# A deformable convolution, attention and experts in one kernel: each image's offset convolutions move among its own sampling steps, and two expert tiles are loaded earlier

## The chip, the cores and the metric

The kernel is one launch on one core of a Trainium2 chip. A core has five engines that run their own instruction streams: TensorE (PE, matrix products), VectorE (DVE), ScalarE (ACT), GpSimd (POOL) and SyncE (SP, which here only issues transfers). Sixteen DMA engines move data between device memory and the core's SBUF, and the products land in PSUM. The metric is the device time of the launch in microseconds.

## The reference, cut to what matters

The input is four images of 256 channels and 64 x 64 pixels, all in float32. The computation is

```
x = x + deform_conv(group_norm(x))       # 3 x 3, modulated, offsets from a convolution
t = tokens(x)                            # 4 x 4096 tokens of 256
t = t + attention(layer_norm(t))         # 8 heads; 4 images attend to each other
t = t + experts(layer_norm(t))           # 8 experts, the best 2 for each token
```

In the deformable convolution, a 3 x 3 convolution over the normalised image gives 27 numbers for each pixel: for each of the nine taps a shift in y, a shift in x, and a mask before its sigmoid:

```
om = conv(x, w_off) + b_off;  off = om[:18];  mask = sigmoid(om[18:])
y, x = pixel + tap + off
sampled = sum over 4 neighbours of (weight of the neighbour) * img[neighbour] * mask
out = sum over 9 taps and channels of w_conv * sampled
```

This convolution is called the offset convolution below, and the arithmetic that turns its 27 numbers into a row index and four weights for each tap is called the positions.

## The kernel before, in words

**The sampling loop** is the first stage. An image is 32 rows of 128 pixels, and each row has nine taps, so an image has 288 steps and the loop has 1,152. For each image there is a table in device memory in which one row of 4 KB holds the four neighbours of a place. In step n, an indirect transfer (`gather`, L626, issued by POOL) brings 128 such rows into one of ten buffers, ten steps ahead. `corner0` (L643, ACT) takes the first neighbour times its weight, `corner` (L651, DVE) adds the other three, `turned` (L665, PE) transposes the sum, `to_sbuf` (L671, ACT) copies it out of PSUM and `product` (L690, PE) multiplies it with the tap's weights. A row's nine taps gather in one PSUM bank; `done` (L699, L701) copies it out and stores four rows at a time. The gathers are issued in pairs, and each pair waits for the last corner sum that still reads one of its buffers.

**The preparation of an image** is cut into small pieces by `pieces(b)`, and each piece has a step number at which it is issued. The loop issues, after its own instructions of step n, what is due at n (`todo`). On DVE, ACT, PE and POOL the order of issue is the order in the program, so a piece stands exactly between two steps; SP's order is chosen by the framework. The pieces are:

- group norm: 16 statistics (L332) at steps 32 to 47 and a few small operations, done at step 56.
- `block(q, at)`, for each of eight blocks of 512 pixels. `norm` (L395) normalises the block. With `table`, `turn` and `leave` (L402, L415, L421) transpose it and store it into the table. With `offsets`, `rows_of` (L433) makes six products, `shifted` (L445) copies them with the bias, `summed` (L454) adds the three shifted rows up and `kept` (L463) copies the 27 numbers out. With both, one normalised tile, of the block and a row above and below it, serves both.
- `positions` (L509 to L556), 16 DVE pieces and one mask on ACT.

Image 0 is prepared before the loop, except for the offset convolutions and positions of blocks 2 to 7. Those stand among image 0's own steps, at 12 + 36 (q - 2), two positions a step, and are done 17 steps before the gathers need them. Images 1 to 3 are prepared in whole during the image before: the eight blocks with table and offsets come every 22 steps (`PERIOD`) from step 56, and then one set of positions over all 32 rows, one operation a step, at steps 235 to 250.

**Memory.** The stages share SBUF through pools that are opened and closed in turn. A tile that lies where an earlier one lay waits for the last use of the earlier one. The two input images in use are `a_x0` and `a_x1`, side by side; the temporaries of the positions are in `a_tmp`.

**The attention** follows in two passes over the eight blocks. In the second, `block(j)` (L1291 on), the order on all engines but POOL is written out by hand, and `chore` slips in the loading of the experts' weights (`experts_in`), the plan of the experts' tiles (`plan`) and their padding rows (`fill`). The tokens are scattered to the experts' rows in device memory as they become ready. The states of blocks 0 to 4 lie in one tile, `early_state`; when those blocks are done, the experts' weights take 10,256 of its 20,480 columns.

**The experts** follow: 142 tiles of 256 tokens. `fetch(n)` reads the tile's first row from the plan into a register of SP and loads the tile into one of five buffers `xt`; `turned_in` (L1556) transposes it on PE, `hidden` (L1577) and `result` (L1595) are the two products, and `weights1` and `weights2` copy the expert's weights. Three tiles are fetched ahead. The `xt` buffers lie where the tiles of the attention's second pass lay.

Of the kernel before, what the change touches and what calls it, by code (L numbers as in the profile page):

```python
# [17 lines left out]
P = 128  # L18
# [3 lines left out]
K2 = 9  # L22
# [23 lines left out]
EARLY = 2  # L46
PERIOD = 22
# [22 lines left out]
XTS, YS = 5, 4  # L70
NG = B * NT
# [7 lines left out]
def conv_attn_moe_kernel(  # L79
# [145 lines left out]
    with ExitStack() as actx:  # L225
# [10 lines left out]
            actx.enter_context(tc.tile_pool(name=f"a_x{i}", bufs=1)) for i in range(2)  # L236
# [80 lines left out]
        def pieces(b):  # L317
# [49 lines left out]
            om = atmp.tile([P, NR, NOFF], F32, name=f"om{b}", tag="om") if b else None  # L367

            def block(q, at, table=True, offsets=True, alone=False):
# [89 lines left out]
                def kept():  # L459
                    of[q] = om[:, rows_in(q), :] if b else atmp.tile(  # L460
                        [P, NT, NOFF], F32, name=f"om{b}_{q}", tag="om_", bufs=2
                    )
                    V.tensor_copy(of[q], t["pt"])  # L463
# [110 lines left out]
            if b:  # L574
                for q in range(NBLK):
                    block(q, n + q * PERIOD)
                n += (NBLK - 1) * PERIOD + 25
                later.append((n - 1, place_for))
                later.extend(positions(slice(0, NR), lambda: om, n, 1))
                assert n + 16 <= STEPS - AHEAD, n  # L580
                return later
# [3 lines left out]
            place_for()  # L585
            for q in range(NBLK):
                first.extend(block(q, n + 10 * q, offsets=False, alone=True))
            n += 10 * NBLK + 8
            for q in range(EARLY):
                at = n + 20 * q  # L590
                first.extend(block(q, at, table=False, alone=True))
                first.extend(positions(rows_in(q), lambda q=q: of[q], at + 25, 4))
            router = routed(
                [wconv_sb[:, ch, k, :] for ch in range(NCH) for k in range(K2)],
                wconv_sb[:, :, :, C:], rwc_sb, ps_tp, ps_om, asm, "wconv",
            )
            for m in range(NCH * K2 + 2):
                first.append((n + 10 + 1.5 * m, lambda: next(router)))
            for q in range(EARLY, NBLK):
                at = (q - 2) * NT * K2 + 12  # L600
                block(q, at, table=False)
                later.extend(positions(rows_in(q), lambda q=q: of[q], at + 25, 2))
                assert at + 33 <= q * NT * K2 - AHEAD, q
# [1189 lines left out]
```

## Time and profile before

| | us |
|---|---|
| median of three runs | 3588.42 |
| lowest and highest run | 3581.35, 3590.16 |
| the profiled execution | 3621.63 |
| its span, first to last instruction | 3619.9 |
| sampling of image 0, 1, 2 (first L671 to first L671) | 522.9, 504.9, 506.6 |
| sampling of image 3 | 512.9 |
| attention, both passes | 791.0 |
| experts and output | 701.0 |

| image | TensorE busy | DVE | ACT | POOL | granted clock | DMA share | GB/s |
|---|---|---|---|---|---|---|---|
| 0 | 468.5 | 392.4 | 291.2 | 306.5 | 0.95 | 0.90 | 320 |
| 1 | 438.1 | 376.4 | 270.5 | 324.8 | 0.94 | 0.92 | 339 |
| 2 | 437.9 | 376.6 | 269.9 | 330.4 | 0.95 | 0.91 | 331 |
| 3 | 402.5 | 354.2 | 231.9 | 345.4 | 0.88 | 0.83 | 297 |

Busy times are microseconds within the image's stretch. The clock is the share of full speed that TensorE was granted; the DMA share is the mean busy share of the sixteen DMA engines. A line of the timeline has the start, the length, the engine, the line of the kernel, the operation, what it writes and reads, a count of instructions merged into it, and in brackets how long the engine stood idle before it and what ended that. In a table of windows the last three columns are the clock, the DMA share and the rate.

### The profile page before, as it was taken

What the parts mean: (1) busy time and instruction counts of PE and PEld (TensorE: products, weight loads), DVE (VectorE), ACT (ScalarE), POOL (GpSimd) and SP (SyncE); (2) the same over time, 40 slices, a digit from 0 to 9 for tenths busy, and PEclk for the clock granted to TensorE, in tenths of its full rate; (3) what the DMA queues carried; (4) which work ended last, traced back from release to release, by engine and by line L of the source; (5) the groups of instructions that cost most, each with busy time, mean ns of one, the idle gap of its engine ahead of it and who ended that gap; (6) DMA issues with size and microseconds to landing.
All of it is one profiled execution on the core that took longest, in us unless ns stands there. A gap on an engine that the chain in (4) does not pass through costs nothing.

```text
span 3619.9 us, 49496 instructions
## 1 busy us (share of the span) xinstructions
PE 3041.8 (84%) x13658; PEld 2230.4 (62%) x13658; DVE 2480.5 (69%) x6303; ACT 1832.4 (51%) x4281; POOL 1961.6 (54%) x1818
## 2 busy tenths in 40 slices
PE   5899997899987899977777889997676588899996
PEld 4667665667665676656566655543343367788884
DVE  5867686777776777866666758875445555455887
ACT  2556554456554565544444457744344254455663
POOL 2555565666576665677666643305445536655441
PEclk8999998999998999989888989998788789999996
DMA  9889889899989899988787878723234334444888
GB/s 301 306 304 336 316 326 351 278 353 366 348 313 350 307 346 341 352 297 310 280 312 285 320 205 141 139 74 121 99 105 154 111 97 132 154 138 153 289 280 285
DMA packets 349897, 911.66 MB, mean 252 GB/s; under 512 B 43540, under 2 KB 123035, under 8 KB 347576
## 3 DMA queue, kind: packets, MB, share of 16 engines
q0 software_dynamic: 208704, 689.10, 55.1%
q1 hardware_dynamic: 140920, 219.39, 19.0%
q8 instruction: 113, 1.85, 0.2%
q14 instruction: 160, 1.31, 0.1%
HBM read 741.87 MB, written 170.12 MB: 252 GB/s over the span
## 4 chain that ended last, share of the span: by engine, by line
PE 48%; issue 14%; POOL 11%; DMA 9%; DVE 8%; another core or an unknown queue 6%; ACT 3%; SPq 0%; POOLq 0%; DVEq 0%; ACTq 0%
PE acc L690 13%; POOL g L626 10%; DMA g<-table,idx 6%; PE ph L1577 6%; PE py L1595 5%; PE tps L665 3%; PE po L433 3%; PE po L1129 3%; DVE s L651 3%; PE p_wq_sb L796 3%; PE p_wk_sb L796 3%; PE pg L796 2%; PE pv L796 1%; DVE mix L1098 1%
## 5 line engine op out<-in xcount | busy, mean ns | idle before, releaser
L651 DVE SCALAR_TENSOR_TENSOR s<-g,wts,s 128x256 f32<-128x256 f32 x3456 | 1433.5, 479 | 542.3 <-ACT s L643 374.3
L626 POOL DMA_INDIRECT g<-table,idx x1152 | 1310.4, 1137 | 765.7 <-DVE s L651 465.2
L690 PE MATMUL acc<-wconv_sb,sT 128*128 128x265 f32 x4608 | 1338.9, 415 | 274.3 <-ACT sT L671 165.7
L690 PEld LDWEIGHTS acc<-wconv_sb,sT 128*128 128x128 f32 x4608 | 832.4, 201 | 423.5 <-ACT sT L671 196.2
L671 ACT COPY sT<-tps 128x256 f32<-128x256 f32 x1152 | 425.4, 369 | 781.0 <-PE tps L665 489.9
L643 ACT ACTIVATE s<-g,wts 128x256 f32<-128x256 f32 x1152 | 588.9, 511 | 210.2 <-DMA g<-table,idx 180.9
L665 PE MATMUL tps<-ident,s 128*128 128x128 f32 x2304 | 461.7, 283 | 39.8 <-DVE s L651 37.8
L665 PEld LDWEIGHTS tps<-ident,s 128*128 128x128 f32 x2304 | 327.7, 148 | 270.1 <-issue 162.4
L1606 POOL DMA_INDIRECT ys_rows<-y,to x284 | 282.9, 996 | 299.9 <-DVE y L1603 225.2
L1577 PE MATMUL ph<-xT,w 128*128 128x256 f32 x1136 | 282.8, 392 | 35.6 <-DVE second L1563 18.3
L1273 POOL DMA_INDIRECT xs_rows<-u,slots x256 | 250.0, 976 | 94.6 <-issue 88.8
L1595 PE MATMUL py<-w,hT 128*128 128x256 f32 x1136 | 270.7, 381 | 0.0
L1581 ACT ACTIVATE hT<-ph,w 128x256 f32<-128x256 f32 x284 | 132.7, 474 | 237.2 <-PE ph L1577 170.0
L1577 PEld LDWEIGHTS ph<-xT,w 128*128 128x128 f32 x1136 | 210.3, 196 | 66.6 <-ACT hT L1581 18.4
L1600 DVE TENSOR_TENSOR y<-py,w 128x512 f32<-128x512 f32 x142 | 98.2, 691 | 206.8 <-ACT w L1539 70.7
L1595 PEld LDWEIGHTS py<-w,hT 128*128 128x128 f32 x1136 | 218.3, 192 | 30.5
L1098 DVE SCALAR_TENSOR_TENSOR mix<-pv,att,mix 128x512 f32<-128x512 f32 x192 | 131.0, 742 | 142.6 <-remote 106.3
L1103 ACT ACTIVATE gate<-pg,bg_c 128x512 f32<-128x512 f32 x64 | 43.8, 688 | 277.1 <-DVE mix L1118 190.1
L919 DVE SCALAR_TENSOR_TENSOR junk<-q,k 128x512 f32<-128x512 f32 x256 | 162.1, 687 | 24.6 <-ACT k L900 24.4
L433 PE MATMUL po<-xs,woff_sb 128*96 128x512 f32 x288 | 152.4, 612 | 0.0
L796 PE MATMUL pg<-early_state,wg_sb 128*128 128x512 f32 x160 | 87.1, 680 | 76.9 <-DVE mix L1098 61.8
L1178 POOL TENSOR_TENSOR rstd<-l3var,nhalf 128x8 f32<-128x8 f32 x16 | 26.5, 1656 | 215.1 <-DVE l3var L1176 207.2
(264 smaller groups left out, 3432.1 us busy)
## 6 DMA issues: line engine op xcount, KB each, us to landing
xt<-xs_rows SPq DMA_DIRECT2D x142, 260.0 KB
table<-zt SPq DMA_DIRECT2D x96, 256.0 KB
yk<-ys_rows SPq DMA_DIRECT2D x80, 256.0 KB
g<-table,idx POOLq DMA_INDIRECT x1152
t<-o SPq DMA_DIRECT2D x32, 530.0 KB
t<-bo_sb POOLq DMA_DIRECT2D x32, 530.0 KB
dt<-t SPq DMA_DIRECT2D x64, 265.0 KB
xraw<-in_x SPq DMA_DIRECT2D x16, 1024.0 KB
```

Source lines behind the costliest of these rows:

```text
L433: T.matmul(t["po"], woff_sb[:, ch, ki].rearrange("p kj o -> p (kj o)"), t["xs"][:, ch, ki : ki + RB], start=(n == 0), stop=(n == NCH * 3 - 1),
L626: g = G.indirect_dma_start(out=gs[n % NGB], out_offset=None, in_=tables[b], in_offset=bass.IndirectOffsetOnAxis(ap=params[b][0][:, r, k : ...
L643: first = S.activation(ss[n], gs[n % NGB][:, :C], AF.Copy, scale=params[b][1][:, 0, r, k : k + 1])
L651: last_corner[n] = V.scalar_tensor_tensor(ss[n], gs[n % NGB][:, c * C : (c + 1) * C], params[b][1][:, c, r, k : k + 1], ss[n], ALU.mult, A ...
L665: T.transpose(tps[n][:, ch * P : (ch + 1) * P], s[:, ch * P : (ch + 1) * P], ident)
L671: S.copy(sTs[n], tps.pop(n))
L690: T.matmul(accs[n // K2][:, :CR], sT[:, ch * P : (ch + 1) * P], wconv_sb[:, ch, k, :], start=False, stop=(k == K2 - 1 and ch == NCH - 1),)
L796: T.matmul(ps, w[:, ci, ch * P : (ch + 1) * P], src[:, ci, :], start=(ci == 0), stop=(ci == NCH - 1),)
L1273: s = G.indirect_dma_start(out=rows_, out_offset=bass.IndirectOffsetOnAxis(ap=slots[:, k, n : n + 1], axis=0), in_=u[:, n % NT, :], in_off ...
L1577: T.matmul(ph, w1_sb[:, ch, f * P : (f + 1) * P], xT[:, ch, :], start=(ch == 0), stop=(ch == NCH - 1),)
L1595: T.matmul(py[:, i, :], hT[:, f, i * P : (i + 1) * P], w2_sb[:, f, :], start=(f == 0), stop=(f == NCH - 1),)
L1606: s = G.indirect_dma_start(out=ys_rows[g], out_offset=bass.IndirectOffsetOnAxis(ap=to[:, i : i + 1], axis=0), in_=y[:, i, :], in_offset=No ...
```

## The change

For images 1 to 3 the preparation during the image before keeps the group norm, the eight table blocks (still every 22 steps from 56) and, of the offset convolutions, only those of blocks 0 and 1, at steps 212 and 232 (`EARLY_AT`), each followed by its own positions. The offset convolutions and positions of blocks 2 to 7 stand among the image's own steps, as those of image 0 did already. So a table block and an offset block no longer share a normalised tile, and the tile for all 32 rows' 27 numbers is gone. One of the two input images now lies at the other end of SBUF.

In the experts, `fetch` is defined inside the attention's second pass. The first two tiles are fetched there, after the last block, into the columns of `early_state` behind the weights; the other tiles use `xt` as before.

```diff
+EARLY_AT = 212
+SOONER = 2
-            actx.enter_context(tc.tile_pool(name=f"a_x{i}", bufs=1)) for i in range(2)
+            actx.enter_context(tc.tile_pool(name=f"a_x{i}", bufs=1, side=("left", "right")[i]))
+            for i in range(2)
...
-            om = atmp.tile([P, NR, NOFF], F32, name=f"om{b}", tag="om") if b else None
...
-            if b:
-                for q in range(NBLK):
-                    block(q, n + q * PERIOD)
-                n += (NBLK - 1) * PERIOD + 25
-                later.append((n - 1, place_for))
-                later.extend(positions(slice(0, NR), lambda: om, n, 1))
+            else:
+                later.append((n - 1, place_for))
+                for q in range(NBLK):
+                    block(q, n + q * PERIOD, offsets=False)
+                for q in range(EARLY):
+                    at = EARLY_AT + 20 * q
+                    block(q, at, table=False)
+                    later.extend(positions(rows_in(q), lambda q=q: of[q], at + 25, 2))
             for q in range(EARLY, NBLK):
                 at = (q - 2) * NT * K2 + 12
+                at += STEPS if b else 0
                 block(q, at, table=False)
                 later.extend(positions(rows_in(q), lambda q=q: of[q], at + 25, 2))
...
+        def fetch(n):
+            g, q = tiles[n]
+            row = nc.sync.value_load(plans[g][1][0:1, q : q + 1], min_val=0, max_val=NE * CAP)
+            if n < SOONER:
+                at = NE * WROW + n * NTB * ROW
+                xts[n] = early_state[:, at : at + NTB * ROW].rearrange("p (t c) -> p t c", c=ROW)
+            else:
+                xts[n] = mt.tile([P, NTB, ROW], F32, name=f"xt{n}", tag="xt", bufs=XTS)
...
         while chores:
             chore()
+        for n in range(SOONER):
+            fetch(n)
...
-        for n in range(FETCH):
+        for n in range(SOONER, FETCH):
             fetch(n)
```

## The prediction

> **What bounds the kernel now.** I read the slices of the page first, to see which resource is full in which stage; then the stages by the count of sampling steps; then the timeline inside one slow and one quick stretch; then the hand-over to the experts. The sampling loop fills some 2,050 us of the span of 3,619.9 us, and the first 23 of the page's 40 slices:
>
> ```profile
> PEclk8999998999998999989888989998788789999996
> DMA  9889889899989899988787878723234334444888
> GB/s 301 306 304 336 316 326 351 278 353 366 348 313 350 307 346 341 352 297 310 280 312 285 320 205 141 139 74 121 99 105 154 111 97 132 154 138 153 289 280 285
> ```
>
> The DMA engines are nearly full there and the rate swings between 278 and 366 GB/s. Every step gathers 128 rows of 4 KB, 0.524 MB, so the loop is a gather loop, and a stage at 300 GB/s is losing something. Which stages lose is seen by counting steps: L671 (the copy of a sampled tile out of PSUM) runs once a step, so its count in a window is the number of steps. Columns: window, length, busy time of L671 with its count, granted TensorE clock, DMA share, GB/s.
>
> ```profile
> 212.50:475.60 263.10, 53.31 (x144) 0.97 0.92 325
> ...
> 534.00:603.50 69.50, 13.31 (x36) 0.83 0.84 303
> ...
> 739.90:977.70 237.80, 53.40 (x144) 1.00 0.97 358
> ...
> 1034.10:1108.40 74.30, 13.13 (x36) 0.79 0.84 313
> ...
> 1239.90:1483.70 243.80, 53.46 (x144) 0.99 0.96 348
> ...
> 1540.60:1615.00 74.40, 13.21 (x36) 0.85 0.82 299
> ...
> 1630.90:2021.00 390.10, 78.33 (x213) 0.87 0.84 299
> ```
>
> In order: steps 72 to 216 and the last 36 of image 0; the same two of image 1; the same two of image 2; steps 12 to 225 of image 3. Length over count is the pace: 1.83, 1.93; 1.65, 2.06; 1.69, 2.07; 1.83 us a step. Image 3 has no preparation work left beside its steps, and yet it is slower than images 1 and 2, which prepare a whole image beside theirs. The timeline says why. First the end of image 1's whole-image position work, then the middle of image 3:
>
> ```profile
> 1032.68 9.58 DVE L651 SCALAR_TENSOR_TENSOR s<-g,wts,s 128x256 f32<-128x256 f32 x24
> 1033.89 9.20 POOL L626 DMA_INDIRECT g<-table,idx  x1 [0.30 <-issue]
> ...
> 1729.94 11.97 DVE L651 SCALAR_TENSOR_TENSOR s<-g,wts,s 128x256 f32<-128x256 f32 x30 [0.22 <-ACT s L643]
> ...
> 1733.93 7.61 POOL L626 DMA_INDIRECT g<-table,idx  x1 [0.30 <-issue]
> 1741.85 0.95 POOL L626 DMA_INDIRECT g<-table,idx  x1 [0.30 <-issue]
> ...
> 1745.59 0.88 DVE L651 SCALAR_TENSOR_TENSOR s<-g,wts,s 128x256 f32<-128x256 f32 x2 [3.68 <-ACT s L643]
> ```
>
> A gather's issue takes 0.95 us, but 9.20 and 7.61 us when the VectorE runs its corner sums without a gap, 24 or 30 in a row; it ends when the row of sums ends. Meanwhile no new transfer starts, the buffers empty, and the VectorE then sits idle (3.68 us) for data that was issued late. Ten landed buffers make the next row of sums without a gap, and so it repeats. Steps that are held up a little by other work (a convolution on TensorE) leave gaps, and the gathers go out evenly: 358 GB/s.
>
> [...]
>
> **The change, part by part.** The sums are made against the profiled execution: 3,621.63 us, span 3,619.9. The median of the runs is 3,588.42, a factor of 0.991, with which I scale at the end.
>
> Durations come from these groups of the loop (busy, mean ns, then idle before):
>
> ```profile
> L433 PE MATMUL po<-xs,woff_sb 128*96 128x512 f32 x288 | 152.4, 612 | 0.0
> ...
> L454 PE MATMUL pt<-tap_sum,oc 96*128 96x27 f32 x256 | 34.6, 257 | 1.9 <-ACT oc L445 1.8
> ...
> L395 ACT ACTIVATE xs<-xraw,nb,rs 128x640 f32<-128x640 f32 x36 | 33.4, 926 | 0.0
> ...
> L509 DVE TENSOR_TENSOR pos<-om,grid 128x576 f32<-128x576 f32 x3 | 2.3, 751 | 0.0
> ...
> L509 DVE TENSOR_TENSOR pos<-om,grid 128x72 f32<-128x72 f32 x8 | 1.8, 226 | 0.1
> ```
>
> *Convolutions moved.* Thirty of the 32 blocks run inside the loop before and after, but as 14, 8, 8, 0 in images 0 to 3 before and 8, 8, 8, 6 after. One block is twelve L433 records at a pitch of 0.43 us (5.2 us) and eight of L454 (1.0 us): 6.2 us of TensorE. Image 0 sheds six (37 us of TensorE work), image 3 takes six, and within images 1 and 2 they come every 36 steps plus two at steps 212 and 232, where they came every 22.
>
> - Image 0, steps 72 to 216: its 263.1 us become the pace of images 1 and 2 there, 1.65 or 1.69. I take 1.69: -20 us. Bounds: 0 (stays at 1.83) and -26.
> - Images 1 and 2, steps 72 to 216: 481.6 us at 1.67 go to 1.69, +5 us, since the convolutions are sparser. A block with its bias copies, sums and positions occupies 24 of 36 steps, against 16 of 22 now, so the cover is nearly as dense (67% against 73%). Bounds: 0 and +46 (all at image 3's present 1.83).
> - Image 3, steps 12 to 225: 390.1 us at 1.83. What remains to be moved is 0.539 MB a step (a gather and the output rows), 1.51 us at 358 GB/s. I take 1.69, about the middle of 1.83 and 1.51: -30 us. Bounds: -68 and, if the six blocks simply lengthen the path, +37.
>
> *Whole-image positions removed.* Sixteen steps of images 0 to 2 each carried one operation on all 32 rows, 9.0 us of VectorE an image, and the gather of 9.2 us came right after them. The last 36 steps take 69.5, 74.3 and 74.4 us; at image 3's uncovered pace of 1.83 they would take 65.9 each: -21 us. Bounds 0 and -36 (1.69).
>
> *Operations added.* Twenty-one more sets of 17 small operations on VectorE: 24 blocks at 3.6 us (the 17 small groups sum to 28.5 us for eight blocks) less 27 us, +58 us over 864 steps, 0.07 us a step. VectorE is busy 354 of 513 us in image 3 and 376 of 505 in image 1: I cost it at nothing; without that cover it is 58 us. ScalarE gets 48 more normalisations at some 0.81 us (926 ns for 640 elements, 869 for 576, taken on to 512) and 21 masks: 44 us, on an engine busy 232 to 291 us an image. Behind each stand one corner product, issued three steps ahead, and one copy; at most 0.9 us late, covered by that lead.
>
> *Queues.* Six memsets of border rows move in POOL's order from steps 56 and 210 to 212 and 192; the readers they wait for ended four steps earlier, so no gather waits. On SP five weight loads move from the end of image 2 to behind the 24th output store of image 3 and wait for the last temporaries (step 225); the next store behind them is at step 253, and their reader at the end of the loop. Nothing.
>
> *First two tiles of the experts.* The hand-over now:
>
> ```profile
> 2917.95 0.69 DVE L1146 TENSOR_TENSOR st<-po,dt 128x512 f32<-128x512 f32 x1 [0.94 <-PE po L1129]
> 2918.91 4.86 SPq L1531 DMA_DIRECT2D xt<-xs_rows  x5
> ...
> 2922.24 2.10 PE L1556 MATMUL tpx<-ident,xt 128*128 128x128 f32 x8 [4.33 <-DMA xt<-xs_rows]
> ...
> 2924.16 3.49 PE L1577 MATMUL ph<-xT,w 128*128 128x256 f32 x8
> ```
>
> SP waits 6.0 us for the last L1147 because the tile buffers lie under attention's. In state space long free the two loads go at once, some 6 us earlier; TensorE transposes at about 2918. The next thing is then ScalarE's copy of the first weights (2920.07, 0.65 us): L1577 starts at 2920.8 instead of 2924.16, -3.4 us; I take -3. Tile 2 keeps its present issue at 2918.9 and lands about 2922.2, before it is needed.
>
> Sum: -20 + 5 - 30 - 21 - 3 = -69 us: a span near 3,551; scaled, 3588.42 - 68 = 3,520 us.
>
> **Rivals.** *Nothing gained, work only moved.* If the convolutions lengthen the path wherever they stand, image 3 pays 37, image 0 gets back at most 22 (its pace can't pass image 1's), the last steps give 21 and the tiles 3: -9 us, 3,579. For it: in image 3 TensorE already takes part in long waits. Against it: images 1 and 2 carry eight blocks at a better pace than image 3 with none. *Slower: sparse cover doesn't break the rows of sums.* Between two blocks 12 steps are bare, and a row of sums needs about ten steps to shut the gathers out. If that returns every 36 steps, all the covered stretches, 645 steps and 1,134.8 us now, run at 1.83: +46; and if the last 36 steps gain nothing either, with -3: +43 us, 3,631; with their gain, 3,610. It decides from a mean pace of 1.796 us a step up (1,134.8 + 24 over 645). *Faster than I say:* if the gathers run evenly to the end, image 3 goes to 1.51 (-68), image 0 gets -26, the last steps -36: about -130 us, 3,460.
>
> **From this to the numbers.** Two times within 0.3% I can't tell apart here. Chances: my forecast, between -35 and -100 us, 0.62; the faster case, 0.12; work only moved, 0.14, whose -9 us lie near the bound of 11 and which I split 0.05 faster and 0.09 the same; slower, 0.12, of which 0.02 stay within the bound. That gives faster 0.79, same 0.11, slower 0.10. The range 3,465 to 3,590 reaches from most of the faster case to the case of moved work and leaves the slower one out; the forecast's own range is 3,488 to 3,553.
>
> **What would show it.** Right: image 3's steps 12 to 225 near 1.69 us with over 320 GB/s and a clock over 0.93; gathers over 2 us there down from a dozen to half; image 0 near 490 us; no gather of 9 us after step 250 of images 0 to 2; the first L1577 about 3 us after the last L1146. Wrong: images 1 and 2 above 1.75 us a step between 72 and 216, or the gathers of image 3 as long as now beside TensorE rows that are merely longer.

## The result, and the profile after

The changed kernel takes 3,642.69 us (median of four runs, 3,633.57 to 3,644.8), the kernel before 3,589.29: a ratio of 1.0124, 95% interval 1.0089 to 1.016. It is slower by some 53 us, where I forecast 69 us less.

The two profiled executions are nearer to each other than the medians: 3,644.8 us (span 3,643.1) against 3,621.63 (span 3,619.9). The one of before ran 32 us over its median, so the stretches below are read for their pattern, and a second pair, further down, has to confirm it.

First the same three rows of slices of the page. The changed kernel no longer has the slices of 353 and 366 GB/s in image 1 (slices 9 and 10), and image 3 (slices 18 to 23) gains little:

```profile
PEclk8999999999998999988999899999778889999996
DMA  9898899898989898988888878724325334444888
GB/s 306 310 320 317 318 327 345 306 327 321 319 321 350 301 328 312 335 307 289 308 297 308 310 236 149 140 55 146 115 79 163 120 97 132 149 141 145 292 282 288
```

Then the same stretches, counted by the copy of a sampled tile (now L675). Columns: window, length, busy time with the count of steps, clock, DMA share, GB/s.

```profile
206.70:475.20 268.50, 52.95 (x145) 0.94 0.89 318
538.30:603.90 65.60, 13.25 (x36) 0.90 0.88 327
730.80:994.80 264.00, 52.96 (x144) 0.93 0.91 323
1058.50:1122.00 63.50, 13.34 (x37) 0.87 0.89 336
1256.40:1517.50 261.10, 53.07 (x144) 0.95 0.91 326
1581.20:1643.40 62.20, 13.24 (x36) 0.89 0.80 295
1672.00:2046.30 374.30, 78.39 (x213) 0.93 0.86 305
```

The middle of images 1 and 2 went from 237.8 and 243.8 us to 264.0 and 261.1, at 323 and 326 GB/s instead of 358 and 348. The last 36 steps of images 0 to 2 and the middle of image 3 are quicker. So the gains that were expected are partly there, and a loss of 43.5 us in images 1 and 2, which was priced at 5, outweighs them, together with 18.9 us in steps 216 to 252, which were not priced at all (the table further down has every stretch).

What is new in images 1 and 2 is seen in the timeline of image 1, at the end of a block's positions (L526 is the last of them; L655 is the corner sums, L630 the gathers):

```profile
746.99 0.94 POOL L630 DMA_INDIRECT g<-table,idx  x1 [2.32 <-DVE s L655]
747.03 0.19 DVE L526 TENSOR_TENSOR wts<-hi,lo 128x36 f32<-128x36 f32 x1
747.14 0.19 DVE L526 TENSOR_TENSOR wts<-lo 128x36 f32<-128x36 f32 x1
747.24 6.03 DVE L655 SCALAR_TENSOR_TENSOR s<-g,wts,s 128x256 f32<-128x256 f32 x15
...
748.24 1.10 POOL L630 DMA_INDIRECT g<-table,idx  x1 [0.30 <-issue]
...
749.64 4.45 POOL L630 DMA_INDIRECT g<-table,idx  x1 [0.30 <-DVE s L655]
...
753.69 1.28 DVE L655 SCALAR_TENSOR_TENSOR s<-g,wts,s 128x256 f32<-128x256 f32 x3 [0.42 <-ACT s L647]
```

Two position operations a step, with no convolution beside them, put VectorE behind ScalarE: over the 24 sets of blocks 2 to 7, a step's first sum starts a median of 0.69 us after ScalarE's product for it has ended, and 0.03 us in the eight steps before a set. When the set ends, VectorE catches up in one unbroken row of 15 sums (6.03 us): within it a step's first sum starts up to 1.11 us after its product, at the step behind it 0.04 us. The third gather of that row takes 4.45 us and ends 0.82 us behind the row's last sum, near the 0.95 us of an undisturbed gather. The same stands at a fixed place behind every set: of the 144 gathers of each such stretch (gather n is that of step n, and is issued ten steps before it), numbers 91, 127, 163 and 199 of an image (or the neighbour) take 4.4 to 5.9 us, in images 0, 1 and 3 all four, in image 2 three. Before, none of the 288 in images 1 and 2 took over 2.5 us. I call those over 2.5 us late.

What it costs is in the groups of instructions of that window alone (steps 72 to 216 of image 1; busy, mean ns, idle before). Before:

```profile
L651 DVE SCALAR_TENSOR_TENSOR s<-g,wts,s 128x256 f32<-128x256 f32 x432 | 179.7, 480 | 55.5 <-ACT s L643 27.8 <-issue 14.0 <-ACT zt L415 7.4
L626 POOL DMA_INDIRECT g<-table,idx x144 | 147.9, 1027 | 89.9 <-DVE s L651 55.0 <-issue 34.9
L643 ACT ACTIVATE s<-g,wts 128x256 f32<-128x256 f32 x144 | 73.7, 512 | 0.4
```

After:

```profile
L655 DVE SCALAR_TENSOR_TENSOR s<-g,wts,s 128x256 f32<-128x256 f32 x432 | 180.2, 479 | 75.3 <-ACT s L647 51.9 <-issue 18.2 <-ACT sT L675 2.1
L630 POOL DMA_INDIRECT g<-table,idx x144 | 162.5, 1128 | 100.9 <-DVE s L655 70.2 <-issue 30.4 <-DMA g<-table,idx 0.3
L647 ACT ACTIVATE s<-g,wts 128x256 f32<-128x256 f32 x144 | 73.6, 511 | 12.8 <-DMA g<-table,idx 10.1 <-DVE s L655 1.6 <-issue 0.9
```

The sums themselves take the same 180 us. The gathers take 14.6 us more; ScalarE's first corner product, which waited 0.4 us in all, now waits 12.8, 10.1 of them for gathered data; VectorE waits 20 us more. Over the two stretches of images 1 and 2, VectorE is busy 376.17 us where it was 360.48, and idle 148.9 where it was 121.1. So of the +43.5 us, 15.7 are work that was added to VectorE and 27.8 are idle time. Its gaps of over 1.5 us grow more than that, from 42.9 to 91.7 us, while the short ones shrink; of the 91.7 us, 50.2 stand at a late gather's own step or the nine behind it.

Over the whole loop the time that gathers take beyond 0.95 us is the same in both (219.6 and 220.7 us). It was not made more, it was moved: it fell from 64.1 to 39.3 us in steps 12 to 225 of image 3, where VectorE had been idle 158.7 us of 512.9 over the image, and from 47.9 to 31.7 in the last 36 steps of images 0 to 2; it rose from 35.9 to 74.6 in their steps 72 to 216, which had been more even.

The hand-over to the experts went as forecast:

```profile
2941.17 1.48 SPq L1518 DMA_DIRECT2D early_state<-xs_rows  x2
...
2946.14 1.04 PE L1567 MATMUL tpx<-ident,early_state 128*128 128x128 f32 x8
2946.34 0.69 DVE L1150 TENSOR_TENSOR st<-po,dt 128x512 f32<-128x512 f32 x1 [0.94 <-PE po L1133]
...
2949.37 1.99 PE L1588 MATMUL ph<-xT,w 128*128 128x256 f32 x8 [2.19 <-ACT w L1550]
```

From the last sum of the attention (L1150) to the first product (L1588) it is 3.03 us; before it was 6.21 (2917.95 to 2924.16).

### The profile page after: what moved, and what is told of

Its sections match the earlier page's. It is cut to its first block, busy times and chain, and to the rows that moved or that the text cites. A ratio compares the mean times of both kernels' runs of the same rounds, so it can differ in the third digit from the quotient of the medians.

```text
span 3643.1 us, 49906 instructions
## 1 busy us (share of the span) xinstructions
PE 3058.8 (84%) x13658; PEld 2237.6 (61%) x13658; DVE 2512.4 (69%) x6660; ACT 1858.1 (51%) x4350; POOL 1960.6 (54%) x1818
## 3 DMA queue, kind: packets, MB, share of 16 engines
q1 hardware_dynamic: 140920, 219.39, 18.9%
## 4 chain that ended last, share of the span: by engine, by line
PE 53%; issue 13%; DVE 9%; POOL 7%; DMA 7%; another core or an unknown queue 6%; ACT 4%; SPq 1%; ACTq 0%; POOLq 0%; DVEq 0%
PE acc L694 16%; POOL g L630 6%; PE ph L1588 6%; PE py L1606 5%; DMA g<-table,idx 5%; PE tps L669 4%; PE po L435 4%; DVE s L655 3%; PE p_wq_sb L800 3%; PE p_wk_sb L800 3%; PE po L1133 3%; PE pg L800 2%; PE pv L800 2%; DVE mix L1102 1%
## 5 line engine op out<-in xcount | busy, mean ns | idle before, releaser
L655 DVE SCALAR_TENSOR_TENSOR s<-g,wts,s 128x256 f32<-128x256 f32 x3456 | 1439.5, 479 | 538.5 <-ACT s L647 388.0
L630 POOL DMA_INDIRECT g<-table,idx x1152 | 1310.3, 1137 | 801.2 <-DVE s L655 512.4
L675 ACT COPY sT<-tps 128x256 f32<-128x256 f32 x1152 | 424.2, 368 | 828.8 <-PE tps L669 468.8
L1588 PE MATMUL ph<-xT,w 128*128 128x256 f32 x1136 | 278.4, 388 | 38.9 <-DVE second L1574 17.3
L1588 PEld LDWEIGHTS ph<-xT,w 128*128 128x128 f32 x1136 | 207.2, 193 | 69.1 <-ACT w L1550 20.0
L1606 PEld LDWEIGHTS py<-w,hT 128*128 128x128 f32 x1136 | 219.6, 193 | 31.0
L1133 PE MATMUL po<-wo_sb,mix 128*128 128x265 f32 x512 | 124.0, 401 | 12.3 <-DVE s L1151 12.3
```

Of the source, the lines that this page charges most:

```text
L630: g = G.indirect_dma_start(out=gs[n % NGB], out_offset=None, in_=tables[b], in_offset=bass.IndirectOffsetOnAxis(ap=params[b][0][:, r, k : ...
L655: last_corner[n] = V.scalar_tensor_tensor(ss[n], gs[n % NGB][:, c * C : (c + 1) * C], params[b][1][:, c, r, k : k + 1], ss[n], ALU.mult, A ...
L675: S.copy(sTs[n], tps.pop(n))
L1133: T.matmul(po[:, n, :CR], o[:, ch, i * P : (i + 1) * P], wo_sb[:, ch, :], start=(ch == 0), stop=(ch == NCH - 1),)
L1588: T.matmul(ph, w1_sb[:, ch, f * P : (f + 1) * P], xT[:, ch, :], start=(ch == 0), stop=(ch == NCH - 1),)
L1606: T.matmul(py[:, i, :], hT[:, f, i * P : (i + 1) * P], w2_sb[:, f, :], start=(f == 0), stop=(f == NCH - 1),)
```

## The experiments

There are eighteen runs, each beside the kernel before on the same chip; every ratio below is to that, with its 95% interval. The sets of runs are of two kinds. In some the kernel before takes 3,545 to 3,594 us, like the one of the prediction; I say that they ran on slow chips. In others it takes 3,138 to 3,139 us; I say quick chips. Whether the chip itself or something else about a set makes the difference was not looked into. Before's own profile on a quick chip moves 373 GB/s in the sampling loop against 321, at a granted clock of 0.98 against 0.93.

My first theory (theory 1 in the texts below) was that the crowded sets of positions make VectorE catch up in unbroken rows, which shut the gathers out. The rivals: that the convolutions stand too far apart to break the rows (theory 2); that they lengthen the path by their own work on TensorE; that the loss comes from the early tiles; and that the long gathers have nothing to do with VectorE's rows.

**Which half of the change.** The convolutions alone (after, with no early tile), and the early tiles alone:

```diff
-SOONER = 2
+SOONER = 0
```

> The change without the early expert tiles (none is fetched before the experts' stage). If the sampling loop holds the whole loss, this is slower than before by 50 to 60 us, 3 us more than the whole change, so near 3,645 us. If the early tiles cost something, it is nearer to before than the whole change: under 3,630 us.

For the second, `fetch` of the changed kernel with its two early tiles, put into the kernel before and nothing else:

> The kernel before with the two early expert tiles alone. By the working of the prediction 3 us faster than before, near 3,586 us, which lies inside the spread of the runs; the first expert product starts about 3.4 us nearer to the last attention sum. If the early tiles cost something, 3,595 us or more.

And the kernel before once more, for a trace of it on this chip:

> The kernel before, unchanged, profiled a second time. Its profiled execution took 3,621.6 us where the other runs took 3,581 to 3,592. If that was a chance of the one execution, this profile spans about 3,590 us, and the stages that shrink say where the 32 us were. If profiling itself costs this kernel 32 us, it spans 3,620 us again.

On a quick chip (before 3,139.40) the convolutions alone take 3,160.08, 1.0070 [1.0045, 1.0095]; the tiles alone 3,138.81, 0.9991 [0.998, 1.0002]; before again 1.0003 [0.9989, 1.0017]. So the loss is that of the convolutions and positions. The interval of the tiles holds both their 3 us (0.9990) and nothing; in the traces, from the last attention sum to the first expert product it is 3.53 us with them and 6.65 in before again.

This chip also showed what I hadn't known to ask. The loop there isn't short of data: in the trace of before again, VectorE's gaps of over 1.5 us sum to 3.1 us in steps 72 to 216 of images 1 and 2 and to 3.6 in image 3, which takes 391.3 us. There the convolutions and positions take 30.5 us from image 0 and add 11.4, 3.9 and 36.4 to images 1, 2 and 3 (stretches of the two traces): nearly the rival of moved work, in which six blocks simply lengthen image 3's path.

**One position operation a step instead of two**, on the changed kernel, over 16 steps instead of 8 (the line stands twice, for early and later blocks):

```diff
-                later.extend(positions(rows_in(q), lambda q=q: of[q], at + 25, 2))
+                later.extend(positions(rows_in(q), lambda q=q: of[q], at + 25, 1))
```

> The change with the positions of a block spread over 16 steps, one operation a step, where they were two a step over 8. Theory 1, the sets of position operations put VectorE behind and its catching up shuts out the gathers: half the extra work a step, so the long gathers after each set (now 5.8 us at the same place of every 36 steps) shrink or go, and the time falls by 20 to 50 us, to 3,595 to 3,620 us. Theory 2, the sparse convolutions are to blame: the long gathers stay and the time stays within 10 us of 3,643.

3,112.89 us on the quick chip, 0.9897 [0.9871, 0.9924]: better than before, and 47.2 us less than the convolutions alone in the same set, of which 3 may be the tiles. The two loops (the columns behind the length are busy time and count of PE, PEld, DVE, ACT and POOL, then clock, DMA share and GB/s), convolutions alone first:

```profile
81.70:1867.40 1785.70, 1665.76 (x8477) 1270.83 (x8475) 1532.72 (x4073) 1101.64 (x2753) 1285.98 (x1165) 0.98 0.97 368
81.40:1825.90 1744.50, 1649.65 (x8478) 1269.62 (x8476) 1518.15 (x4073) 1101.01 (x2753) 1213.16 (x1165) 0.99 0.99 377
```

VectorE has the same 4,073 instructions; of the 41.2 us, 14.6 are busy time and 26.6 idle. Late gathers go from 21 to 11. Again, on a slow chip (before 3,593.53):

> The change with a block's positions one a step, a second time, in the hope of a chip on which the kernel before takes 3,540 us or more, since the chip of the first set took 3,139. On such a slow chip: if the crowding of two operations a step does the harm, 0.990 to 1.000 of before, like the run without positions (0.999) or better; if the mere amount of small operations does it, 1.01 or more, as the change. On a quick chip again about 0.990.

3,563.52, 0.9919 [0.989, 0.9948]. The gathers of that run, whole loop:

```profile
L630 POOL DMA_INDIRECT g<-table,idx x1152 | 1206.1, 1047 | 815.9 <-DVE s L655 523.9
```

1,206.1 us against 1,310.3 of the changed kernel; seven gathers of over 2.5 us against 32. Same operations, same places of the convolutions, only spread. What that is worth on a slow chip can't be read from this run, since the crowded kernel did not run in its set: the change took 1.0124, 1.0141 and, as the second pair below shows, 0.9935 of before in three sets on slow chips, and the last is as good as this one's 0.9919 [0.989, 0.9948]. So that spreading gains is shown on a quick chip alone. Nor does it return what was lost in images 1 and 2: their steps 72 to 216 take 254.5 and 254.8 us here, against 481.6 for both in the first trace of before.

**Without the positions.** Blocks 2 to 7 of images 1 to 3 get no positions; row r then uses the indices and weights of row r mod 8, so the other instructions stay, though the gathers read the same places again:

```diff
-                later.extend(positions(rows_in(q), lambda q=q: of[q], at + 25, 2))
+                if b == 0:
+                    later.extend(positions(rows_in(q), lambda q=q: of[q], at + 25, 2))
...
+        def row_of(b, r):
+            return r % (EARLY * NT) if b else r
```

> The change with the positions of blocks 2 to 7 of images 1 to 3 left out; their steps use the indices and weights of blocks 0 and 1. The convolutions stay. Theory 1, the sets of position operations cause the long gathers: those at 91, 127, 163 and 199 are gone from images 1 to 3 and stay in image 0; the time falls below before, by 1% or more against the whole change. Theory 2, the sparse convolutions let the rows of sums come back: the long gathers stay, within 0.4% of the whole change.

**Without the convolutions.** The same blocks get no normalisation and no convolution; their positions are worked out from zeros, so the gathers read unshifted places:

```diff
+                bare = b > 0 and q >= EARLY and not table
...
-                    V.tensor_copy(of[q], t["pt"])
+                    V.tensor_copy(of[q], nothing if bare else t["pt"])
...
+                if bare:
+                    out_.append((at + 24, kept))
+                    return out_
```

> The change with the offset convolutions of blocks 2 to 7 of images 1 to 3 left out (normalisation, products, copies, sums); their positions are worked out from zeros. Theory 1: the long gathers at 91, 127, 163 and 199 stay in images 1 to 3. Theory 2: with no convolution the gathers behave as in image 3 of the kernel before, with no long ones at these four places in particular. Beside this the time shows what 18 convolutions cost on the path: if 6.2 us of TensorE each lie on it, about 110 us less than the whole change; if they are hidden, under 30 us.

Beside both ran the changed kernel again, on a slow chip where before takes 3,544.94:

> The whole change, unchanged, beside the others of this set. On the chip of the first set, where the kernel before takes 3,139 us, the change without the early tiles was 0.7% slower; with the tiles, which gave 0.1%, I expect 0.5 to 0.7% slower on such a chip, and 1.2% on one like the first, where the kernel before takes 3,589 us. In images 1 to 3 the gathers issued just after a block's positions (numbers 91, 127, 163, 199) take 3.5 to 6 us.

After again 3,593.90, 1.0141 [1.0119, 1.0164]; without positions 3,547.24, 0.9992 [0.9973, 1.0011]; without convolutions 3,602.08, 1.0166 [1.0145, 1.0186]. Taking the positions out returns 46.7 of the 49.0 us; taking out 18 convolutions, over 100 us of TensorE work at 6.2 us each, returns nothing. So on this chip either TensorE's work isn't on the path, or the gaps that it makes are worth as much as it costs. What the other addresses of the gathers do to these two times was not separated.

The first result has two readings: the late gathers that went, or the work that VectorE no longer did. The loops of the two traces, after again and without positions, columns as above:

```profile
80.00:2101.10 2021.10, 1737.23 (x8478) 1321.55 (x8478) 1531.82 (x4075) 1092.74 (x2753) 1311.42 (x1165) 0.94 0.91 326
79.60:2050.80 1971.20, 1722.94 (x8476) 1317.86 (x8474) 1491.06 (x3767) 1091.21 (x2735) 1260.81 (x1165) 0.95 0.92 334
```

VectorE's busy time falls by 40.8 us of the 49.9, its idle time by 9.1. In steps 72 to 216 of images 1 and 2 the busy time is 17.5 of 18.2, though of seven gathers of 4.4 to 5.8 us there only one so long (6.4 us) is left. So this pair does not show that the lateness cost the time; the operations' own time can account for most of it. Against their own time as the whole price stands the quick chip, where the same operations, spread, took 47.2 us less.

In the trace without positions, of the gathers of steps 72 to 216 of images 1 to 3 only one takes over 3 us (6.4); in image 0, whose positions stand as in the changed kernel, three of the four behind its sets are as long as ever. Without convolutions long gathers stay in every image, up to 9.4 us.

**The row, or what a sum reads: the running sum in PSUM.** Each corner sum reads two tiles of SBUF, `g` and `s`. The question is whether the gathers go free when one of the two lies elsewhere. The running sum goes to PSUM, and only the third corner writes SBUF; two of the transposes' four banks are given up for it:

```diff
-        ps_tp = actx.enter_context(tc.tile_pool(name="ps_tp", bufs=4, space=PSUM))
+        ps_tp = actx.enter_context(tc.tile_pool(name="ps_tp", bufs=2, space=PSUM))
...
-            ss[n] = asm.tile([P, C], F32, name=f"s{n}", tag="s")
+            ss[n] = sums[n % 4 // 2][:, n % 2]
...
+                of, to = ss[n], ss[n]
+                if c == 3:
+                    to = ss[n] = asm.tile([P, C], F32, name=f"sf{n}", tag="s")
                 last_corner[n] = V.scalar_tensor_tensor(
-                    ss[n], gs[n % NGB][:, c * C : (c + 1) * C],
-                    params[b][1][:, c, r, k : k + 1], ss[n], ALU.mult, ALU.add,
+                    to, gs[n % NGB][:, c * C : (c + 1) * C],
+                    params[b][1][:, c, r, k : k + 1], of, ALU.mult, ALU.add,
```

On the changed kernel, with the slow chip of the last three:

> The change with the running corner sums in PSUM, so that the first two of a step's three corner operations read one SBUF tile and the third writes the sum to SBUF; the transposed tiles get two PSUM banks where they had four. [...] no gather takes over 2.5 us, whatever VectorE's rows are, and the time falls by 1% or more, unless two banks slow TensorE. If the long gathers have another cause (a full queue of transfers), they stay.

3,433.44, 0.9687 [0.9656, 0.9718]. Its gathers and first two corner sums, from the page:

```profile
L660 DVE SCALAR_TENSOR_TENSOR sums<-g,wts,sums 128x256 f32<-128x256 f32 x2304 | 1101.4, 486 | 169.3 <-ACT sums L649 81.5
L632 POOL DMA_INDIRECT g<-table,idx x1152 | 1086.9, 944 | 816.4 <-DVE sf L660 434.1
```

A mean of 944 ns over 1,152 gathers (1,141 in after again), none over 2.5 us, and 0.6 us in all beyond 0.95 each. Then on a quick chip (before 3,137.63), on both kernels, and the two banks by themselves, where the long gathers should stay if it isn't the banks that free them:

> The kernel before with the running corner sums in PSUM, as in the run on the change, and two PSUM banks for the transposed tiles. No gather over 2.5 us. If the change's own merit was only hidden by the shut-out gathers (convolutions spread over the images), this is slower than the changed kernel with its sums in PSUM by 10 to 30 us, most of it in image 0 with its 14 convolutions. If the change has no merit of its own, the two are equal or this is the faster.

> The changed kernel with the running sums in PSUM once more, so that it stands beside the kernel before with the same edit on one chip. About 3% faster than before on a chip where the kernel before takes 3,540 us or more; on a chip like that of the first set (3,139 us) less, 1 to 2%.

> The change with two PSUM banks for the transposed tiles instead of four, the sums left in SBUF[...]. [...] the long gathers stay as in the change and the time is the change's or up to 1% more. If fewer banks pace the loop and so help, it is faster than the change and its long gathers go.

Sums in PSUM on the kernel before: 3,196.92, 1.0194 [1.0174, 1.0214]; on the changed kernel 3,219.65, 1.0269 [1.0247, 1.029]; the banks alone 3,168.09, 1.0098 [1.0079, 1.0118], with long gathers as in the changed kernel. So the banks aren't what frees the gathers; and on a quick chip the free gathers are worth less than they cost, where I had expected a gain of 1 to 2%. The cost is seen in the start-to-start time of two sums: 0.396 us in a row with both in SBUF, a median of 0.515 with the sum in PSUM.

That also leaves a second reading, the looser rows. With both in SBUF each sum of a row starts 0.08 us before the one ahead has ended; with the sum in PSUM most start only after it has (the median of 0.515 against a length of 0.48 to 0.49), as here in the changed kernel on the quick chip, with 0.10 us between the two lines:

```profile
1701.26 1.01 DVE L660 SCALAR_TENSOR_TENSOR sums<-g,wts,sums 128x256 f32<-128x256 f32 x2
1702.37 0.48 DVE L660 SCALAR_TENSOR_TENSOR sf<-g,wts,sums 128x256 f32<-128x256 f32 x1
```

The edit takes an input out of SBUF and loosens the rows, and no run does one without the other.

One more thing is read from this pair. No gather is late in either kernel, and still the changed one takes 22.7 us more than the kernel before, as the convolutions alone did with sums in SBUF (20.7). So a loss of that size on a quick chip needs no late gathers. On a slow chip again, on the kernel before (before 3,593.53):

> The kernel before with its running sums in PSUM, on another chip. On a slow chip: if the change has a merit of its own that the shut-out gathers hid, this is over 0.969 of before, the ratio of the changed kernel with this edit on a slow chip; if the change has none, it is 0.969 or less. On a quick chip about 1.019 again.

3,501.45, 0.9739 [0.9696, 0.9781].

With sums in PSUM the two kinds of chip come nearer: the loop of the changed kernel so altered takes 1,875.0 us on the slow chip and 1,849.5 on the quick one, 1.4% apart, where the kernel before takes 2,047.3 and 1,764.3, 16% apart. At 1.63 us a step the slow chip delivers 350 GB/s. But the kernel before with the same edit takes 1,931.6 and 1,818.2 us in the loop, 6% apart, with no gather late on either. So late gathers are not all that a slow chip loses by.

**Small sets beside dense convolutions.** If crowded sets alone were the cause, they should hurt the kernel before too. There each block's positions were put right behind its convolution, two a step, with the convolutions still 22 steps apart (the temporaries of images 1 to 3 also get places of their own):

```diff
+                later.append((n - 1, place_for))
                 for q in range(NBLK):
                     block(q, n + q * PERIOD)
-                n += (NBLK - 1) * PERIOD + 25
-                later.append((n - 1, place_for))
-                later.extend(positions(slice(0, NR), lambda: om, n, 1))
+                    later.extend(positions(rows_in(q), lambda q=q: of[q], n + q * PERIOD + 25, 2))
```

> The kernel before with its convolutions where they are, every 22 steps in the image ahead, but each block's positions in small operations, two a step, right behind its convolution, in place of one set over all 32 rows. Theory 1: small sets alone do the harm, so images 0 to 2 get long gathers after each set and are slower by 10 us or more an image in steps 72 to 216, less about 9 us for the set over all rows; in sum slower than before by 0.3 to 1%. Theory 2, it is the sparser convolutions: no long gathers there, and 10 to 25 us faster than before, since the 9.2 us gather after the large set goes.

> The kernel before with small sets of positions right behind convolutions every 22 steps, a second time; on the quick chip it was 0.997 of before, not slower as theory 1 had it. On a slow chip, where shut-out gathers starve the transfers: theory 1 gives 1.003 to 1.010 of before, with long gathers behind each set. If it is 0.997 or less there too, small sets do harm only where the convolutions stand further apart than 22 steps, and the cause is the two together. On a quick chip 0.997 again.

3,127.65 on a quick chip, 0.9966 [0.9956, 0.9975], and 3,590.06 on a slow one, 0.9990 [0.997, 1.001]. My first theory alone is missed by both: the same crowded sets do no harm here. The time includes what is gained with the one large set gone, but steps 72 to 216 of images 1 and 2, where that never stood, say the same: 440.2 us on the quick chip, 437.9 in before again on another. A block's six products stand at its steps 4 to 16 and its set at 25 to 32. With blocks 22 steps apart, the set lies at steps 3 to 10 of the next block, among its products; with blocks 36 apart, the next product is eight steps behind the end of the set. The gathers fit that: behind the sets of images 1 to 3 they are on time or take 3.2 to 3.5 us, except behind the last set of an image, which no convolution follows: there four of six, in the two traces, take 8.2 to 9.4 us. In these runs long gathers behind the sets take both, the crowd and steps without a convolution's products behind it.

**Both cures together**, sums in PSUM and one operation a step, on the changed kernel (slow chip, before 3,593.66):

> The change with both edits: one position operation a step, and the running sums in PSUM. If the crowded sets cost time only by shutting gathers out, spreading them gives nothing more here: on a slow chip 0.965 to 0.972 of before, as with the sums in PSUM alone, on a quick chip 1.02 to 1.03. If the crowding costs VectorE time of its own, it is 0.5% or more below these.

3,423.22, 0.9521 [0.9494, 0.9548]: 170 us less than before beside it, and the best that was measured on a slow chip. It is 1.7% below the 0.9687 of the sums in PSUM alone, so by what was expected the crowding costs time of its own beside the late gathers; but that run was of another set. It wasn't run on a quick chip, where sums in PSUM by themselves lost time.

**A second pair of traces.** Since the first trace of before was 32 us over its median, both kernels ran once more, side by side:

> The kernel before, profiled once more, in the hope of a slow chip. The prediction was summed on an execution 32 us above the median of its runs. If that execution is typical of such a chip but for chance, the stretches agree with it within some 5 us each; if its image 3 was unusually starved, image 3 takes 15 us or more less here, and the forecast gain in image 3 was measured from too high a start.

> The change, profiled beside the kernel before on the same chip, so that the stretches can be compared pair by pair. On a slow chip: steps 72 to 216 of images 1 and 2 longer by 15 to 25 us each, image 0's by 0 to 8, image 3 within 15 us of before, the last 36 steps of images 0 to 2 shorter by 4 to 12 each.

Before 3,580.30, 0.9982 [0.9948, 1.0015] to the other runs of before (3,585.80); after 3,566.20, **0.9935** [0.9899, 0.9971]. On this slow chip the change is a gain. That was in no theory of mine. Image 3 of before, steps 12 to 225, takes 397.6 us here, so the 390.1 that the prediction started from was not unusually high. The two pairs, by stretch:

| stretch | forecast | first pair | second pair |
|---|---|---|---|
| image 0, steps 72 to 216 | -20 | +5.4 | -4.1 |
| images 1 and 2, steps 72 to 216 | +5 | +43.5 | +26.6 |
| image 3, steps 12 to 225 | -30 | -15.8 | -32.0 |
| last 36 steps of images 0 to 2 | -21 | -26.8 | -37.4 |
| steps 216 to 252 of images 0 to 2 | 0 | +18.9 | +13.8 |
| the rest of the loop | 0 | +9.4 | +14.9 |
| the loop | -66 | +34.6 | -18.2 |

The stretches have the same signs in both but for image 0; the sizes decide the sign of the sum. In images 1 and 2, steps 72 to 216, VectorE's busy time goes from 361.40 to 376.44 us in the second pair and its idle time from 109.9 to 121.6; its gaps of over 1.5 us go from 30.3 to 61.1. What makes one slow chip pay 44 us there and another 27 is not settled.

## Why the prediction was wrong, step by step

*Images 1 and 2, steps 72 to 216: "+5 us", the cover being "nearly as dense (67% against 73%)".* This is the step that failed, together with the next. It was +43.5 and +26.6, the first near the bound of +46 that I gave and then didn't believe. I counted the steps that have any other work in them, but the work is of two kinds. Convolutions on TensorE came with gaps between the corner sums: before, the longest unbroken row is 12 and 18 sums in these stretches of images 1 and 2, with a convolution every 22 steps, and 39 in image 3, steps 12 to 225, with none. Position operations stand on VectorE itself: they take its time (15.7 of the 43.5 us, 15.0 of the 26.6), they put it behind (0.69 us against 0.03), and the catching-up is a row without a gap (the 15 sums above). The sets cover no steps; right behind them, in steps without a convolution, stand the late gathers (numbers 91, 127, 163 and 199 or the neighbour, 4.4 to 5.9 us). That the late gathers make up the rest, 27.8 and 11.7 us of idle time, is argued from where the long gaps stand; the sparser convolutions may have a part in it. My 24 steps of 36 had the 8 steps of the set in them. Without these the cover is 16 of 36, 44% against 73%.

*"Operations added": "I cost it at nothing; without that cover it is 58 us".* The second half of the same error. That VectorE has idle time was my reason, and it doesn't hold: VectorE was busy 32.8 us more over the loop (1,532.35 against 1,499.53), and its idle time did not shrink for it (549.6 against 547.8). The price was measured: 46.7 us for the positions of 18 blocks on a slow chip, 2.6 us a block, where I had put the whole of a block's time at 3.6 and its cost at nothing. It isn't the duration alone: on a quick chip the same operations, spread, take 47.2 us less. How the price on a slow chip divides between the operations' time and the late gathers stays open.

*Steps 216 to 252, and what follows.* I priced no change there: +18.9 and +13.8. The two early blocks of the next image at steps 212 and 232, with their own sets, and the block at step 192 come together there. The last of these sets, at steps 257 to 264, is followed by a late gather again (number 275, up to 9.4 us), and image 3's first twelve steps take 28.6 us instead of 15.9 (29.0 instead of 17.5 in the second pair). In my sum "the last 36 steps" had a line, and the 36 before them had none.

*Image 0, "-20 us": wrong.* +5.4 and -4.1 on slow chips, since the pace it was to take over, that of images 1 and 2, was no longer there. Where VectorE has no long waits (quick chip), image 0 as a whole shed 30.5 us.

*Image 3, "-30 us": right in sign and in one of the pairs in size* (-15.8, -32.0). The path that I gave, convolutions that break the rows, is only half of what is seen: the late gathers went from twelve to six, but 91, 127, 163 and 199 stand among the six (5.8 to 5.9 us). Clock and rate went from 0.87 and 299 GB/s to 0.93 and 305, short of the 320 that I named. On a quick chip, where image 3 was not short of data, the same blocks cost 36.4 us, the +37 of my bound. The 358 GB/s behind my 1.51 us is no floor for the pace either: one slice of before shows 366, and on the quick chip the whole loop moved 373 and image 3 took 1.34 us a step.

*Whole-image positions, "-21 us": right in the first pair's size*, -26.8, and too small for the second's -37.4. The path is in doubt: the 9.20 us gather behind them (number 261) is gone from all three images, but the sets at 257 to 264 put another of 8.0 to 9.4 us in place of it, so its going can't be what was gained. That the size came out is in part luck.

*First tiles, "-3": right*, 3.2 us in the first pair of traces and 3.1 with the tiles alone.

*The rivals.* Nearest in size is "slower: sparse cover doesn't break the rows of sums", to which I gave 0.12, with 3,610 to 3,631 us. By its path it isn't what came: with the same sparse convolutions and the positions left out the time is 0.9992 of before. Its point of decision, a mean of 1.796 us over 645 steps, was passed: (268.5 + 264.0 + 261.1 + 374.3) / 645 = 1.811. In the second pair the same mean is 1.725 (1,112.9 / 645), and there the change gains, as that point says. But the time of 3,642.69 lies above that rival too; it also left out steps 216 to 252 and image 3's first steps. I had rejected it because images 1 and 2 ran evenly with eight blocks each, and I took a row to need ten steps of bare running. A VectorE that had fallen behind needed five: the row of 15 sums, with its gather of 4.45 us.

*The rows.* I had used the unbroken row to explain long gathers, and not asked of the added operations what rows they would lead to. With the sums in PSUM a gather takes a mean of 944 ns against 1,141 on the same chip, and none is late; but as the rows are looser there too, it isn't shown whether the tile moved out of SBUF or the looser row freed them.

*Left open.* Why the change gains on one slow chip and loses on two others. What the late gathers cost, apart from VectorE's added work. Whether the sparser convolutions have a part in what images 1 and 2 lose; no run kept the changed kernel's order with its convolutions 22 steps apart. Whether a long gather goes with the sum's second tile in SBUF or with the unbroken row. And whether the changed kernel's order is worth anything with sums in PSUM on a slow chip: 0.9687 [0.9656, 0.9718] against 0.9739 [0.9696, 0.9781] were measured against different runs of before, and the intervals overlap; on a quick chip it was worth less than nothing, 3,219.65 us against 3,196.92.

## What to carry to other kernels

In a loop whose transfers are issued by GpSimd, price each operation added to VectorE even where VectorE has idle time: here it was busy 32.8 us more, and its idle time did not shrink (549.6 us against 547.8). And ask whether the operation makes VectorE fall behind: here the backlog was worked off in an unbroken row, 15 sums in 6.03 us, and a gather beside it took 4.45 us instead of 0.95. Spread small operations over more steps rather than in crowds (47.2 us less here, on a quick chip), and put them beside work that comes with gaps (small sets beside dense convolutions took 0.9966 and 0.9990 of before). And cover is not one quantity: work that holds an engine back and work that the engine itself must do are counted on opposite sides.

## What the runs showed of the hardware that I had not expected

A long row of sums did not always go with a long gather. On a quick chip, in the middle of image 3 of the kernel before, VectorE runs 48 sums that the timeline merges into one row, and the gathers beside it take 0.95 to 0.98 us:

```profile
1619.79 20.50 DVE L651 SCALAR_TENSOR_TENSOR s<-g,wts,s 128x256 f32<-128x256 f32 x48
...
1620.94 0.95 POOL L626 DMA_INDIRECT g<-table,idx  x1 [0.31 <-DVE s L651]
1622.19 0.96 POOL L626 DMA_INDIRECT g<-table,idx  x1 [0.30 <-issue]
1623.49 0.95 POOL L626 DMA_INDIRECT g<-table,idx  x1 [0.34 <-DVE s L651]
```

48 sums in 20.50 us are 0.427 each, against 0.396 start to start in the row of 15 beside the gather of 4.45 us. Three of them take 1.28 us, as long as ScalarE takes from the end of one first corner product to the next there (1621.03, 1622.31 and 1623.59 us); by my estimate from these numbers, every third sum waits some 0.09 us for that product, and such short gaps may be what lets the gathers out. No run shows it by itself. A quick chip is not free of late ones: with the convolutions alone, 21 gathers take over 2.5 us there, most of them in the same places behind the sets. But VectorE hardly waits for it: its gaps of over 1.5 us in steps 72 to 216 of images 1 and 2 sum to 4.9 us.

Nor were the first gathers beside a row long: in the row of 15 above, the one at 748.24 took 1.10 us and only the next took 4.45. Why it was that one, no run shows.

The chips differ more than any edit here: the same kernel takes 3,138 to 3,139 us on some and 3,545 to 3,594 on others, and an edit that gained 3% on the one kind (sums in PSUM, 0.9687 and 0.9739) lost 2 to 3% on the other (1.0269 and 1.0194). Only the change with its positions spread gained on both kinds (0.9919 and 0.9897).
